# Four seams of a four-layer network: inverse sums by block transpositions, a query bank, queued maxima and reordered pooling products

## Chip, cores and metric

The kernel runs on one core of a Trainium2 chip. The metric is the device time of one execution in microseconds (us); lower is better. The engines are TensorE (PE in the profile; its weight loads are PEld), VectorE (DVE), ScalarE (ACT), GpSimd (POOL) and SyncE (SP), which issues the DMAs. A core has one of each, and they run their own instruction queues in order, held together by semaphores.

## What is computed

The reference sends two images of 512 channels and 64 x 64 pixels, in fp32, through four residual layers. Each adds a function of the group-normalised input (32 groups) to the input:

```python
x = x + _L0_conv_ref(_gn(x), ...)   # local 3x3 attention with pooled keys
x = x + _L1_conv_ref(_gn(x), ...)   # attention on keys sampled at learnt offsets
x = x + _L2_conv_ref(_gn(x), ...)   # mixture of max pools of sizes 1, 3, ... 13
x = x + _L3_conv_ref(_gn(x), ...)   # linear attention with random features
```

The change touches layers 1 and 2. Layer 1, in short, for each of 8 heads of 64 channels:

```python
q   = einsum('oc,bchw->bohw', w_q, x)
off = tanh(w_off2 @ gelu(q[::4, ::4] * w_off1 + b_off1)) * 4
kv  = w_kv @ grid_sample_bilinear(q, grid + off)     # 16 x 16 = 256 keys
out = w_out @ (softmax(q * 64**-0.5 @ k.T) @ v) + b_out
```

The softmax runs over 256 keys; its denominators are sums of exponentials, one for each head and token. Layer 2 takes the mean of each channel, maps the means through two small matrices to one number per channel, and mixes two neighbouring pool sizes by it:

```python
s = relu(w2 @ relu(w1 @ mean(x) + b1) + b2); q_s = clip(floor(s), 0, 5)
out = (s - q_s) * pool[q_s + 1] + (q_s + 1 - s) * pool[q_s] + x
```

A max pool of size 2j+1 is the 3 x 3 maximum applied j times, and the kernel uses that.

## The kernel before

The two images run one after the other, each through the four layers. An image lies in SBUF as `X`, 128 partitions x 4 channel groups (`cc` or `oc`, 0 to 3) x 4096 pixels; a second such tile, `Y`, takes queries, attention results or maxima. A block (`blk`) is 512 pixels, so there are 8 blocks. PSUM has 8 banks of 128 x 512 fp32; most are rented from rotating pools under the name `mm`. An fp32 matmul appears as two MATMUL records (passes).

The order of the instructions on each engine is set by the framework's scheduler: it simulates the program, starts on each engine the instruction that comes earliest in program order among those that are ready, and then adds the semaphores. Where the code says `manual_schedule(engines=...)`, the named engine keeps the program's order. `issue_after(ins)` orders all instructions of its block on the engine of `ins` behind `ins`, without a semaphore.

**Layer 1, start** (`query_and_sample`, from line 1281). Four banks of the pool `pp` (4 in all) hold the first products for the offsets, 256 columns each; Gelu (line 1255) reads them. `acc` is a tile of four banks of its own. Its banks 0 and 1 serve `shift_columns` (lines 992 to 1009), which makes the query bias `bq`, its bank 2 the last moments (`stats_in_steps`, lines 960 to 973). Later all four gather the sampled features (line 1342). The weights are copied to `wq` by GpSimd (line 1317). `query(0)` then makes the first queries: for each channel group 4 matmuls (`project`, line 134) into a bank, and line 1296 adds the bias. Its first bank comes from `pp`.

**Layer 1, attention** (`layer1`, from line 1037). A loop runs over 32 steps (block, channel group), with later stages some steps behind: exponentials (1495 to 1501), products with the values (1510), once per block `inverse_sums` (1514 to 1527), then `divided` (1534 multiplies out the inverses over the channels, 1537 applies them), then the output product of one channel group per step (`add_output`, 1222 to 1232). In `inverse_sums` the sums of the 8 heads lie in one bank `psD`: in each strip of 32 partitions the even rows hold one head's sums, the odd rows the other's, and `divided` uses only the first two rows of each strip.

In the last block each output group is followed by `bn_aggr` (1116), the mean and variance of the group's channels. Between these stand pieces of layer 2's first 3 x 3 maxima (`maxima_across`, `maxima_down`, `across_rows`, lines 1135 to 1164, the last through `spread_max`, line 698), work for VectorE. Then `pool_mixture` (1180 to 1220) makes the mixture's weights from the means: its first matmul is line 1187, its first VectorE instruction 1189.

**Layer 2** (`layer2`, `pool_chunk`, from line 1358). For each channel group, VectorE makes the pools j = 2 to 6 one out of the other, in two steps each: `spread_max` along x into the scratch `h`, then along y into the next pool. Line 698 does the inner columns or rows on VectorE, 699 the two edges on ScalarE. TensorE adds the weighted pools: `product(b, dg, src, j)` (1403) multiplies block b of pool j with a diagonal matrix (1408, ScalarE) into the accumulator bank `accs[b]`.

In the last group (`cc == KC - 1`) VectorE's order is the program's own. There, the group statistics of the first three channel groups, which layer 3 needs, are made alongside, in the accumulator of the last block, `accs[NB - 1]`: `stats_in_steps` is a generator, and its first step (965 to 968) runs after pool 4, its second (970 to 973) after pool 5. Until then the products of the last block are kept in the list `kept`; they are issued at j = 5, after its block 3. GpSimd's power at 973 gives the scale `rstd`, by which line 1433 (ScalarE) scales layer 3's weights.

Of the kernel before, what the change touches and what calls it, by code (L numbers as in the profile page):

```python
# [9 lines left out]
F32 = mybir.dt.float32  # L10
# [923 lines left out]
class Net(General):  # L934
# [22 lines left out]
        for _ in self.stats_in_steps(ks, pp.tile([P, TB], F32, name="mm") if ps is None else ps):  # L957
            pass

    def stats_in_steps(self, ks, ps):  # L960

        nc, mv = self.nc, self.mv
        nmean, rstd, cent, var = (self.stats[:, i, ks] for i in range(4))
        n = ks.stop - ks.start
        nc.tensor.matmul(ps[:, :n], self.grp, mv[:, ks, 0], start=True, stop=True)
        nc.vector.tensor_tensor(cent, mv[:, ks, 0], ps[:, :n], ALU.subtract)
        nc.vector.tensor_tensor(var, cent, cent, ALU.mult)
        nc.vector.tensor_tensor(var, var, mv[:, ks, 1], ALU.add)
        yield
        nc.tensor.matmul(ps[:, KC:KC + n], self.grp, var, start=True, stop=True)  # L970
        nc.scalar.mul(nmean, ps[:, :n], -1.0)
        nc.vector.tensor_scalar(var, ps[:, KC:KC + n], 1e-5, None, ALU.add)  # L972
        nc.gpsimd.tensor_tensor(rstd, var, self.mhalf[:, :n], ALU.pow)  # L973
# [63 lines left out]
    def layer1(self, X, Y, d):  # L1037
# [6 lines left out]
        with tc.tile_pool(name="l1", bufs=1) as sp:  # L1044
# [13 lines left out]
            with tc.tile_pool(name="l1c", bufs=1) as late:  # L1058

                keys = late.tile([P, KC, NK], F32, name="keys")  # L1060
                vals = late.tile([P, 2, C], F32, name="vals")
                with tc.tile_pool(name="l1q", bufs=4, space=PSUM) as pp:
                    for oc in range(KC):
                        ps = pp.tile([P, TB], F32, name="mm")
                        for kc in range(KC):
                            nc.tensor.matmul(ps[:, :NK], wkv[:, kc, oc * P:(oc + 1) * P],
                                             feats[:, kc, :], start=(kc == 0), stop=(kc == KC - 1))
                        nc.scalar.mul(keys[:, oc, :], ps[:, :NK], HD ** -0.5)
                    for t in range(2):
                        ps = pp.tile([P, TB], F32, name="mm")  # L1070
                        for kc in range(KC):
                            nc.tensor.matmul(ps, feats[:, kc, t * P:(t + 1) * P], wkv[:, kc, C:],
                                             start=(kc == 0), stop=(kc == KC - 1))
                        nc.vector.tensor_copy(vals[:, t, :], ps)
                    self.product_bound(top, keys, sp, pp)
                with tc.tile_pool(name="l1b", bufs=2) as wp, \
                        tc.tile_pool(name="l1s", bufs=6, space=PSUM) as pp, \
                        tc.tile_pool(name="l1o", bufs=2, space=PSUM) as ppo:
                    st = wp.tile([P, KC, NB, 6], F32, name="gn_st1", bufs=1)
                    w1 = wp.tile([P, KC, 32], F32, name="w1", bufs=1)  # L1080
                    nc.sync.dma_start(w1, d["w1"].rearrange("(kc p) e -> p kc e", p=P))
                    w2 = wp.tile([32, C], F32, name="w2", bufs=1)
                    nc.sync.dma_start(w2, d["w2"])
                    wo = wp.tile([P, KC, C], F32, name="wo1", bufs=1)
                    nc.sync.dma_start(wo, d["w_out1"].rearrange("(kc p) o -> p kc o", p=P))
                    steps = [(blk, cc) for blk in range(NB) for cc in range(KC)]
                    part = lambda blk, cc=slice(0, KC): Y[:, cc, blk * TB:(blk + 1) * TB]
                    flat = lambda a: a.rearrange("p k o -> p (k o)")
                    probs, totals, later = {}, {}, []
                    rows3 = self.scratch[:, :KC * 10 * W].rearrange("p (k y x) -> p k y x", k=KC, x=W)  # L1090
                    ring = cycle([a[:, n:n + TB] for a, lo, hi in (
                        (flat(wq), 0, KC), (flat(wkv), 5, 8), (flat(feats), 0, 2),
                        (wp.tile([P, 3 * TB], F32, name="totals", bufs=1), 0, 3))
                        for n in range(lo * TB, hi * TB, TB)]).__next__
                    for i in range(len(steps) + 4 + KC):
                        if i < len(steps):
                            blk, cc = steps[i]
                            probs[i], totals[i] = self.exponentials(part(blk, cc), keys[:, cc, :],
                                                                    ring, wp, pp)
                        if 1 <= i <= len(steps):  # L1100
                            blk, cc = steps[i - 1]
                            self.attended(part(blk, cc), probs.pop(i - 1),
                                          vals[:, :, cc * P:(cc + 1) * P], ppo)
                        at = lambda n: i >= n and (i - n) % KC == KC - 1 and (i - n) // KC
                        if (blk := at(1)) is not False and blk < NB:
                            r = self.inverse_sums([totals.pop(KC * blk + n) for n in range(KC)], wp,
                                                  pp)
                        if (blk := at(2)) is not False and blk < NB:
                            self.divided(part(blk), r, pp)
                        if (blk := at(3)) is not False and blk < NB:  # L1110
                            later += [(blk, oc) for oc in range(KC)]
                        if later:
                            blk, oc = later.pop(0)
                            self.add_output(X, wo, part(blk), blk, oc, st, pp)
                            if blk == NB - 1:
                                nc.vector.bn_aggr(self.mv[:, oc, :],
                                                  st[:, oc].rearrange("p b s -> p (b s)"))
                                if oc < 2:
                                    self.maxima_across(X, NB - 2, rows3, slice(oc, oc + 1))
                                    self.maxima_down(Y, NB - 2, rows3, slice(oc, oc + 1))  # L1120
                                for rows in ([(20, 32), (32, 44)], [(10, 20), (44, 55)],
                                             [], [])[oc]:
                                    self.across_rows(Y, slice(*rows))
                            elif oc == KC - 1 and blk < NB - 2:
                                self.maxima_across(X, blk, rows3, slice(0, KC))
                                self.maxima_down(Y, blk, rows3, slice(0, KC))
                    mixture = self.pool_mixture(w1, w2, wp, pp)
                    next(mixture)
                    self.maxima_across(X, NB - 1, rows3, slice(0, 1))
                    self.maxima_down(Y, NB - 1, rows3, slice(0, 1))  # L1130
                    for rows in (0, 10), (55, W):
                        self.across_rows(Y, slice(*rows))
                    next(mixture)

    def maxima_across(self, X, blk, h, ks):
# [145 lines left out]
    def query_and_sample(self, X, Y, wq, bq, grid, feats, top, wp, pp, ppk):  # L1281
# [9 lines left out]

        def query(blk):
            for cc in range(KC):
                ps = pp.tile([P, TB], F32, name="mm")
                self.project(ps, wq[:, :, cc * P:(cc + 1) * P], X, blk)
                nc.scalar.activation(Y[:, cc, blk * TB:(blk + 1) * TB], ps, AF.Identity,
                                     bias=bq[:, cc:cc + 1])
# [88 lines left out]
    def pool_chunk(self, X, Y, cc, c0, d0, wts, sp):  # L1386
# [7 lines left out]
            self.pools.insert(0, Y[:, cc - 1, :])  # L1394
        h = image(self.scratch)
        accs, kept = self.accs, []
        stats = self.stats_in_steps(slice(0, KC - 1), accs[NB - 1])
        if cc == KC - 1:
            self.diags = cycle([next(self.diags), next(self.diags),
                                *[sp.tile([P, P], F32, name=f"diag{i}") for i in range(2, 7)]])  # L1400
# [5 lines left out]
        def add(w, src, j):  # L1406
            dg = next(self.diags)
            nc.scalar.activation(dg, self.ident, AF.Copy, scale=w)  # L1408
            for b in range(NB):
                if b == NB - 1 and cc == KC - 1 and j < 5:  # L1410
                    kept.append((b, dg, src, j))
                else:
                    product(b, dg, src, j)
                while kept and j == 5 and b == 3:
                    product(*kept.pop(0))

        add(c0[:, cc:cc + 1], x2, 0)
        flat = Y[:, cc, :]
        for j in range(1, 7):
            if j > 1:  # L1420
                last, flat = image(flat), self.pools.pop(0)
                self.pools.append(flat)
                if cc or j > 2:
                    self.spread_max(h, last, 2)
                self.spread_max(image(flat), h, 1)
                if cc == KC - 1 and j in (4, 5):
                    next(stats, None)
                if cc == KC - 1 and j == 3:
                    self.moments(sp)
                if cc == KC - 1 and j == 5:  # L1430
# [83 lines left out]
    def inverse_sums(self, totals, wp, pp):  # L1514
# [6 lines left out]
                                 self.cst[:, C_EVEN + h:C_EVEN + h + 32], totals[cc][h],  # L1521
                                 start=(h == 0), stop=(h == 1))
        r = wp.tile([P, TB], F32, name="recip")
        for i in range(2):
            half = slice(i * TB // 2, (i + 1) * TB // 2)
            nc.vector.reciprocal(r[:, half], psD[:, half])
        return r

    def divided(self, att, r, pp):
# [1373 lines left out]
```

## Time and profile before

| what | value |
|---|---|
| median of 3 timed runs | 4915.69 us (4914.85 to 4920.11) |
| profiled execution, its own time | 4912.44 us |
| its span, first to last instruction | 4910.6 us |
| mean granted TensorE clock | 0.989 |
| MATMUL records / VectorE instructions | 16883 / 4044 |
| first image: layer 1, layer 2, layer 3 begin at | 1009, 1482, 1682 us |
| second image: layer 0, 1, 2, 3 begin at | about 2471, 3449, 3917, 4116 us |

The profile's views that are used: the page (busy share of each engine), the list of waits (who waited for whom: total, times, longest), the timeline (start, duration, engine, line, operation, tiles, and in brackets the idle time before it and what ended it), the rows of one line (durations in ns as min/median/max), and tables of stretches (busy time of each engine in a stretch, then the granted clock, the DMA engines' share and GB/s). Times count from the span's start. A wait for several semaphores is put down to the one that came last.

### The profile page before, as it was taken

The page shows a single profiled execution, that of the slowest core. Times are in us where ns is not written, and L with a number is a line of the kernel's source. Part 1 is how long each engine was busy: PE and PEld are TensorE (multiplying, and loading weights), DVE is VectorE, ACT ScalarE, POOL GpSimd, SP SyncE. Part 2 cuts the span into 40 slices and gives each one's busy share as a digit, 9 for nine tenths or more (in the row PEclk, how much of TensorE's full clock was granted, in tenths as well). Part 3 has the DMA queues.
Part 4 walks back from the last instruction along what each step waited for, and adds up shares of the span by engine and source line. Part 5 has one row for each costly group of instructions (what it writes and reads, how often), then busy time and mean ns, then how long its engine had stood idle before and what let it go on. Part 6 is the DMA issues. An engine that isn't in the chain of part 4 may idle for free. (4 is left out here: it accounts for less than half of the span.)

```text
span 4910.6 us, 48474 instructions
## 1 busy us (share of the span) xinstructions
PE 4726.7 (96%) x16883; PEld 1965.5 (40%) x16883; DVE 2983.6 (61%) x4044; ACT 1851.7 (38%) x3555; POOL 1815.6 (37%) x1164
## 2 busy tenths in 40 slices
PE   7999999999999999999999999999999999999999
PEld 3433332555334444433344333325543344444333
DVE  4267777754679633377633677777536795334766
ACT  1256665334323233323212566652443233333222
POOL 0036666501320045545400466665013201454544
PEclk9999999999999999999999999999999999999999
DMA  4035556600000000111120455565000000000111
GB/s 157 1 94 156 154 157 169 178 24 10 1 0 19 1 1 1 56 55 56 65 78 2 108 156 157 156 172 160 20 10 1 2 17 1 1 1 18 44 50 46
DMA packets 129441, 313.30 MB, mean 64 GB/s; under 512 B 23394, under 2 KB 36194, under 8 KB 127652
## 3 DMA queue, kind: packets, MB, share of 16 engines
q1 hardware_dynamic: 129188, 310.12, 21.8%
q8 instruction: 135, 2.21, 0.2%
q14 instruction: 118, 0.97, 0.1%
HBM read 260.73 MB, written 49.31 MB: 63 GB/s over the span
## 5 line engine op out<-in xcount | busy, mean ns | idle before, releaser
L134 PE MATMUL mm<-big,w 128*128 128x512 f32 x2496 | 1157.8, 608 | 19.1 <-DVE big L2485 13.6
L134 PEld LDWEIGHTS mm<-big,w 128*128 128x128 f32 x2496 | 453.1, 191 | 689.7 <-issue 549.0
L2706 POOL TENSOR_TENSOR late<-late,big 128x1024 f32<-128x1024 f32 x194 | 459.2, 2367 | 216.6 <-DVE big L2701 174.4
L1702 POOL TENSOR_TENSOR big<-big 128x512 f32<-128x512 f32 x224 | 277.6, 1271 | 219.3 <-ACT big L1693 219.3
L2526 DVE TENSOR_TENSOR prods<-qs,big 128x2048 f32<-128x2048 f32 (+1 forms) x184 | 330.7, 1819 | 34.3 <-PE tap L2564 23.7
L2701 DVE TENSOR_TENSOR big<-big,mm 128x512 f32<-128x512 f32 x388 | 252.4, 682 | 104.6 <-ACT mm L2693 103.2
L1693 ACT ACTIVATE big<-mm,ed 128x256 f32<-128x256 f32 x512 | 194.1, 490 | 232.7 <-DVE top L1689 200.3
L2693 ACT COPY mm<-big 128x512 f32<-128x512 f32 x432 | 245.4, 597 | 80.3 <-DMA big<-rows 46.1
L2706 POOL TENSOR_TENSOR late<-late,tap 128x1024 f32<-128x1024 f32 x94 | 222.0, 2361 | 97.8 <-DVE tap L2701 83.7
L1501 POOL TENSOR_TENSOR wq<-prob 128x512 f32<-128x512 f32 x48 | 71.9, 1520 | 486.3 <-ACT prob L1498 474.8
L1689 DVE TENSOR_REDUCE top<-mm 128x1 f32<-128x512 f32 x256 | 159.0, 683 | 148.2 <-PE mm L1620 148.2
L2611 POOL TENSOR_TENSOR late<-late 128x512 f32<-128x512 f32 x76 | 95.4, 1275 | 395.7 <-ACT late L2596 379.5
L134 PE MATMUL mm<-big,wq 128*128 128x512 f32 x512 | 235.0, 604 | 2.7 <-ACT off_t L1255 2.7
L1227 PE MATMUL mm<-big,wo 128*128 128x512 f32 x512 | 237.6, 610 | 0.0
L1667 PE MATMUL mm<-w,big 128*128 128x512 f32 x512 | 234.5, 601 | 0.0
L1403 PE MATMUL acc<-big,diag 128*128 128x512 f32 x512 | 227.7, 602 | 5.2 <-ACT diag L1408 4.6
L1961 PE MATMUL mm<-k,w 128*128 128x512 f32 x512 | 232.0, 600 | 0.7 <-DVE big L1964 0.7
L973 POOL TENSOR_TENSOR group_stats<-group_stats,cst 128x1 f32<-128x1 f32 (+1 forms) x20 | 20.2, 1024 | 543.0 <-DVE group_stats L972 489.7
L134 PE MATMUL mm<-big,big 128*128 128x512 f32 x464 | 201.7, 594 | 0.5 <-DVE b_sr L1011 0.5
L1926 POOL TENSOR_SCALAR qf_sum<-qf,ksum_ratio 128x512 f32<-128x512 f32 x64 | 100.4, 1570 | 264.2 <-PE psD L1944 212.4
L1498 ACT ACTIVATE prob<-mm 128x512 f32<-128x512 f32 x256 | 133.3, 602 | 171.3 <-PE mm L1495 171.1
L2564 PE MATMUL tap<-prods,cst 128*32 128x512 f32 x1152 | 183.2, 604 | 11.5 <-DVE prods L2526 7.4
(432 smaller groups left out, 8118.7 us busy)
## 6 DMA issues: line engine op xcount, KB each, us to landing
big<-rows SPq DMA_DIRECT2D x432, 256.0 KB
tap<-rows SPq DMA_DIRECT2D x208, 256.0 KB
yd<-late SPq DMA_DIRECT2D x32, 512.0 KB
lost_all<-lost SPq DMA_DIRECT2D x128, 128.0 KB
out<-big SPq DMA_DIRECT2D x64, 256.0 KB
big<-in_W_kv SPq DMA_DIRECT2D x8, 1024.0 KB
rows<-late SPq DMA_DIRECT2D x64, 128.0 KB
big<-in_x SPq DMA_DIRECT2D x32, 256.0 KB
```

What stands on the lines that cost most here:

```text
L134: self.nc.tensor.matmul(ps, w[:, kc, :], X[:, kc, blk * TB:(blk + 1) * TB], start=(kc == 0), stop=(kc == KC - 1))
L1227: nc.tensor.matmul(ps, w[:, kc, oc * P:(oc + 1) * P], att[:, kc, :], start=(kc == 0), stop=(kc == KC - 1))
L1403: nc.tensor.matmul(accs[b], dg, src[:, b * TB:(b + 1) * TB], start=(j == 0), stop=(j == 6))
L1667: nc.tensor.matmul(ps, X[:, kc, lo:lo + P], wv[:, kc, :], start=(kc == 0), stop=(kc == KC - 1))
L1693: nc.scalar.activation(f[:, t, :], pS[h][i][:, t % 2, :], AF.Exp, bias=ed[:, t, 2 * cc + h:2 * cc + h + 1])
L1702: nc.gpsimd.tensor_tensor(a, a, part, ALU.add)
L1961: nc.tensor.matmul(ps, self.wo[:, kc, oc * P:(oc + 1) * P], qs[:, kc, :], start=(kc == 0), stop=(kc == KC - 1))
L2526: self.nc.vector.tensor_tensor(self.pair(u, k)[:, :n].rearrange("p k (y x) -> p k y x", x=W), bcast(qs.rearrange("p (y x) -> p y x", x=W), ...
L2564: nc.tensor.matmul(ps[32 * q:32 * q + 32, :], self.cst[:, C_TAPW + 16 - 2 * k:][:, :32], self.pair(u, k)[:, 0, j * TB:(j + 1) * TB], start ...
L2693: nc.scalar.copy(ps, part)
L2701: nc.vector.tensor_tensor(part.rearrange("p (y x) -> p y x", x=W), self.vx[:, y:y + self.UY // 2, dx:dx + W], ps.rearrange("p (y x) -> p y ...
L2706: nc.gpsimd.tensor_tensor(out, out, t, ALU.add)
```

## The change

Five edits in four places.

1. `inverse_sums`: the two reciprocals of 256 columns each are replaced by a transposition of `psD` in blocks of 32 x 32, in place; a reciprocal of two columns of each block (16 x 2 = 32 columns); and a transposition back into `r` that reads these two columns 16 times over.
2. `query(0)`: its first product goes into bank 3 of `acc` instead of a bank of `pp`.
3. The two last pieces of `across_rows`, rows 0 to 10 and 55 to 64, are queued on VectorE behind the last `bn_aggr`.
4. `stats_in_steps` has a further stop after its second matmul (line 970), if asked. In the last pooling chunk, both of its matmul steps now stand after pool 4 and ahead of its products; the rest (971 to 973) stands at j = 5 between the two halves of pool 5.
5. The kept products are issued at j = 5 ahead of that pool's own products.

```diff
-    def stats_in_steps(self, ks, ps):
+    def stats_in_steps(self, ks, ps, split=False):
...
         nc.tensor.matmul(ps[:, KC:KC + n], self.grp, var, start=True, stop=True)
+        if split:
+            yield
         nc.scalar.mul(nmean, ps[:, :n], -1.0)
...
-                                nc.vector.bn_aggr(self.mv[:, oc, :],
-                                                  st[:, oc].rearrange("p b s -> p (b s)"))
+                                mean = nc.vector.bn_aggr(
+                                    self.mv[:, oc, :], st[:, oc].rearrange("p b s -> p (b s)"))
...
-                    for rows in (0, 10), (55, W):
-                        self.across_rows(Y, slice(*rows))
+                    with tc.issue_after(mean.ins):
+                        for rows in (0, 10), (55, W):
+                            self.across_rows(Y, slice(*rows))
...
-                ps = pp.tile([P, TB], F32, name="mm")
+                ps = acc[:, KC - 1] if not blk + cc else pp.tile([P, TB], F32, name="mm")
...
-        stats = self.stats_in_steps(slice(0, KC - 1), accs[NB - 1])
+        stats = self.stats_in_steps(slice(0, KC - 1), accs[NB - 1], True)
...
             nc.scalar.activation(dg, self.ident, AF.Copy, scale=w)
+            while kept and j == 5:
+                product(*kept.pop(0))
             for b in range(NB):
                 if b == NB - 1 and cc == KC - 1 and j < 5:
                     kept.append((b, dg, src, j))
                 else:
                     product(b, dg, src, j)
-                while kept and j == 5 and b == 3:
-                    product(*kept.pop(0))
...
+                if cc == KC - 1 and j == 5:
+                    next(stats, None)
                 self.spread_max(image(flat), h, 1)
-                if cc == KC - 1 and j in (4, 5):
-                    next(stats, None)
+                if cc == KC - 1 and j == 4:
+                    next(stats)
+                    next(stats)
...
         r = wp.tile([P, TB], F32, name="recip")
-        for i in range(2):
-            half = slice(i * TB // 2, (i + 1) * TB // 2)
-            nc.vector.reciprocal(r[:, half], psD[:, half])
+        nc.vector.transpose(psD, psD)
+        two = psD.rearrange("p (b n r) -> p b n r", n=16, r=2)[:, :, 0]
+        nc.vector.reciprocal(two, two)
+        nc.vector.transpose(r.rearrange("p (b n r) -> p b n r", n=16, r=2), bcast(two, 2, 16))
         return r
```

## The prediction

> **What bounds the kernel.** I read the page first: the share of each engine, then the clock row. TensorE is busy for nearly the whole span and nothing else comes near, so time is won where TensorE stands still or runs slowly.
>
> ```profile
> PE 4726.7 (96%) x16883; PEld 1965.5 (40%) x16883; DVE 2983.6 (61%) x4044; ACT 1851.7 (38%) x3555; POOL 1815.6 (37%) x1164
> ```
>
> Next the list of who waited for whom, TensorE alone (total us, times, longest). Four of its lines are the places of this change, each met twice, once per image:
>
> ```profile
> PE mm L1187 <- DVE channels_mv L1116: 5.7, 2, 2.8
> PE acc L1403 <- DVE group_stats L972: 5.4, 2, 2.7
> PE mm L1534 <- DVE recip L1526: 4.2, 2, 2.1
> PE mm L134 <- ACT off_t L1255: 2.7, 2, 1.3
> ```
>
> Together 18.0 us, 0.37% of the span. But a stall also costs afterwards. Stretches after the inverse sums of image 0's last block (busy per engine; the number after POOL's is the granted clock):
>
> ```profile
> 1448.00:1449.00 1.00, 0.00 (x0) 0.00 (x0) 1.00 (x1) 0.00 (x0) 0.00 (x0) 1.00 0.00 0
> 1449.00:1450.00 1.00, 0.84 (x8) 0.31 (x8) 0.97 (x3) 0.00 (x0) 0.00 (x0) 0.86 0.00 0
> 1450.00:1451.00 1.00, 1.00 (x5) 0.32 (x2) 0.65 (x2) 0.00 (x0) 0.00 (x0) 0.50 0.00 0
> ...
> 1456.00:1457.00 1.00, 1.00 (x3) 0.50 (x2) 0.00 (x0) 0.00 (x0) 0.00 (x0) 0.73 0.00 0
> ```
>
> After 2.13 us of stall the clock is halved for 0.28 + 6 + 0.54 = 6.8 us. Image 1 has the same stall (2.11) and keeps its clock: from L1534 to the last L1227 it takes 18.50 us, image 0 21.85. So this dip costs 3.35 us. After the L134 stall the first query product likewise takes 5.37 us in image 0 and 3.67 in image 1: 1.70.
>
> **Rule against row.** The Trainium skill, "TensorE: Matmul & The Clock Gate", section "Why this matters for your kernels", asks only that idle gaps stay below about 3 us; by it these gaps of 1.3 and 2.1 us are harmless and parts 1 and 2 lose 5.05 us of worth. The rows show dips, so I count them. The page's Part 1 says that the window (3.4 us) runs freely; that fits one image dipping and the other not, and makes this gain a matter of phase.
>
> **1. Inverse sums.** Two reciprocals at L1526 (1.72 us each, 3.36 for both at 1445.75) become transposition, reciprocal of 32 columns, transposition. The same three stand at L2646 to L2649:
>
> ```profile
> L2646 DVE STREAM_TRANSPOSE mm<-mm x32: 731/731/732, 288.2 to 3371.7; 128x512 f32<-128x512 f32 x32
> ...
> L2648 DVE RECIPROCAL mm<-mm x32: 351/366/367, 289.0 to 3372.9; 128x32 f32<-128x32 f32 x32
> ...
> L2649 DVE STREAM_TRANSPOSE late<-mm x32: 716/717/719, 289.4 to 3373.3; 128x512 f32<-128x512 f32 x32
> ```
>
> 0.731 + 0.366 + 0.717 and two gaps of 0.034 give 1.88: 1.48 less. In 14 of 16 blocks VectorE has slack (psD is ready at 1412.8, L1534 runs at 1420.08), so nothing is won there. In the last block of each image the stall falls from 2.1 to about 0.6: 2 x 1.48 = 2.96, and image 0's dip goes: 3.35. Bound: the two gaps of the chain can take in another instruction, as L1952 enters the chain at L1948 (2.34 us). Only L1230 (0.65) is near ready here; then it is 0.8 per image. I take 1.48, as L1230 comes later in program order.
>
> **2. First query product in a bank of `acc`.** It no longer waits for Gelu (table load 1.28, then 0.56) to free a bank: 1.34 per image, 2.68; its other inputs are ready (last copy of wq ends at 1013.2). It can also fill the 0.75 that TensorE waits for L994 before L1006; between 0 and 0.75 I take 0.5, a bit over one pass of 0.43: 1.0. L1006, bq and Gelu are then up to 0.4 late, covered by the rest of the product (3.4 us). Dip of image 0: 1.70. Sum 5.4. Bank 3 is next written at L1342, well after L1296 has read it.
>
> **3. Maxima's pieces behind the last mean.** At image 0's end of layer 1:
>
> ```profile
> 1470.68 0.80 DVE L698 TENSOR_TENSOR wkv<-big 128x620 f32<-128x620 f32 x1
> ...
> 1471.40 0.74 DVE L1230 SCALAR_TENSOR_TENSOR big<-mm,vec,big 128x512 f32<-128x512 f32 x1
> 1472.06 0.73 DVE L698 TENSOR_TENSOR wkv<-big 128x558 f32<-128x558 f32 x1
> 1472.71 0.69 DVE L1232 BATCH_NORM_STATS2 gn_st<-big 128x6 f32<-128x512 f32 x1
> ```
>
> The last matmul ends at 1471.01. With both pieces gone, L1230, L1232 and L1116 run 1471.08 to 1472.96 (0.75 + 0.69 + 0.37 and gaps) in place of 1473.80: 0.84. The pieces (0.80 + 0.73) now follow the mean. L1189 can start 0.68 to 0.88 after it, so one piece fits (it ends 0.72 after the mean); if both go first, L1189 is 0.5 to 0.7 late. Value between 0.1 and 0.84: 0.4, 0.8 for two. The clock is halved here anyway (the pause is over 8 us).
>
> **4. Last pooling chunk.** TensorE waits from 1660.17 to 1662.86. The named L972 is not the only holder: the product of j = 5 also needs the fifth pool, an L698 that ends at 1662.71.
>
> ```profile
> 1662.86 3.67 PE L1403 MATMUL acc<-pool,diag 128*128 128x512 f32 x8 [2.69 <-DVE group_stats L972]
> 1662.86 4.89 POOL L973 TENSOR_TENSOR group_stats<-group_stats,cst 128x3 f32<-128x3 f32 x1 [185.68 <-DVE group_stats L972]
> ...
> 1667.14 4.29 DVE L698 TENSOR_TENSOR big<-wkv 128x3968 f32<-128x3968 f32 x1
> 1667.78 3.79 ACT L1433 ACTIVATE w<-w,group_stats 128x512 f32<-128x512 f32 x6 [4.56 <-POOL group_stats L973]
> ```
>
> The five kept products (10 passes of 0.429 = 4.3 us) need only L971 and L972. L970 now comes before j = 4's products, so L972 can run at 1658.4, ahead of the fifth pool. Kept products then fill 1660.1 to 1664.4, j = 5 takes 16 passes to 1671.3. Late next is the sixth pool, ready at 1671.43, with j = 6 at about 1671.6 where it is 1674.09: 2.5. One thing takes part of it back: L973 now starts near 1658.7, beside an L698 (4.89 us as today, where the one-column form takes 0.56), so L1433 runs 1663.6 to 1667.4 on ScalarE ahead of the edges of the sixth pool's first half (L699, today 1662.80). Those end at 1667.75, the last L698 starts 0.6 late: 1.9 to 2.0. If L970 stayed behind j = 4's products (1659.89), VectorE would wait 1.9 for L972: 0.6. I take 2.0: 4.0 for two. In layer 2 VectorE runs without a pause of note from 1536 to 1671, so the earlier savings pass through it only because its start (1482) moves with them.
>
> **Sum.** Parts 1 to 4: 6.3 + 5.4 + 0.8 + 4.0 = 16.5. The profiled execution took 4912.44 (span 4910.6 and 1.8 around it) and would take 4895.9. The timed runs' median is 3.25 above it, a difference of the size of one clock dip; I carry it along: 4899.2. Later layers follow TensorE, and no DMA limits a seam (DMA share 0.01 or less in these stretches), so the gains stay.
>
> **Rivals.**
> - Stalls shrink, but the clock takes its share: other seams (1.5 to 1.8 us at 956, 968, 2117, undipped today) meet the windows differently. Without the 5.05: 11.4, 4904.3. For it: one image dips, one doesn't. Against: as many dips can vanish as come.
> - Part 4 turns against itself: POOL's L973 gets through only when VectorE pauses after the next L698 (1667.1); L1433 holds ScalarE to 1671.0, the edges come at 1671.4, the last L698 ends at 1675.8, j = 6 starts 1.8 late. 16.5 - 2 x 3.8 = 8.9: 4906.8. For it: L1433 before the edges in program order; against: L973 needed only one L698 to pass today.
> - Slower: the new chain lets large maxima in. L1143 to L1157 (2.2 to 3.2 us each) enter before it and in both gaps, in the 12 blocks that have them: up to 1.88 + 3 x 3.24 = 11.6 us, against 7.2 from psD to L1534. From 7.2 on TensorE stalls; halfway, 2.7 us in 12 blocks, costs 33: 16 slower, 4932. Against: these maxima end at 1404.7, 8 us before the next psD.
> - That the change does nothing is excluded for part 2: the bank's wait is gone by construction.
>
> **Numbers.** As forecast 0.60 (own range 4895 to 4904), clock rival 0.22, part 4's rival 0.14, slower 0.04. A measurement tells 0.2%, 9.8 us, from no change: the bound is 4905.9. Nearly all of the first case, three quarters of the second and four tenths of the third lie below: faster 0.80, same 0.16, slower 0.04. Low end: fill 1.5, pieces 1.7, part 4 at 5.0 make 18.9, 4896.8, and two dips fewer elsewhere (about 3 each) 4891. High end: third case and a little clock, 4908.
>
> **What would show it.** L134 following L1006 or L994 with no wait on Gelu; L1534's wait near 0.6 and clock 1.00 behind it; L1187's wait near 2.0 to 2.4; kept products at 1660 without a wait, and j = 6 waiting under 1 us on the last L698. L1433 ahead of L699 with VectorE idle, or L1230 within the transpositions, would prove those steps wrong; dips at other seams would make the sum wrong.

## The result, and the profile after

The changed kernel takes 4899.26 us (median of 18 runs, 4895.99 to 4903.53); the kernel before, beside it on the same chip, 4912.43 us (18 runs, 4902.65 to 4920.11). The ratio is 0.9975, 95% interval 0.9969 to 0.9981. By the means of these runs the change is worth 12.6 +- 1.2 us. The profiled execution fell from 4912.44 to 4899.03 us: 13.4.

The page's first line, and then the list of waits of TensorE (total us, times, longest), of the changed kernel:

```profile
PE 4718.9 (96%) x16883; PEld 1963.8 (40%) x16883; DVE 2958.2 (60%) x4060; ACT 1849.4 (38%) x3555; POOL 1815.3 (37%) x1164
```

```profile
PE mm L1190 <- DVE channels_mv L1118: 4.0, 2, 2.0
...
PE mm L2302 <- DMA prods<-yd: 2.9, 4, 1.1
...
PE mm L1197 <- DVE pool_var L1194: 2.8, 2, 1.4
...
PE mm L1541 <- DVE recip L1533: 1.3, 2, 0.6
...
PE acc L1406 <- DVE big L698: 1.0, 2, 0.5
```

TensorE does the same 16883 passes in 7.8 us less busy time: that is half clock that has gone, since a pass at half clock counts double. All lines but L2302's are what the four seams still cost. Two of the old waits are smaller, L1190's (it was L1187's 5.7) and L1541's (it was L1534's 4.2); the 5.4 for the kept products is off the list; three are larger or new: L1197's (L1194's 1.7 before), L1406's on line 698, and L2302's at the output of layer 0, which the change doesn't touch.

To account for all of it I used two sums from the trace: the time between its first and its last matmul in which TensorE runs none, and the time that half clock costs (half of the busy time under a clock record of one half). The span less these two is 4717.7 us before and 4718.4 after, so they explain all but 0.7 of the difference:

| TensorE, both images, us | forecast | before | after | gained |
|---|---|---|---|---|
| 1. inverse sums, idle | 2.96 | 4.23 | 1.25 | 2.98 |
| 2. query bank, idle | 3.7 | 2.67 | 0.83 | 1.84 |
| 3. pieces, idle at two matmuls | 0.8 | 5.68 + 1.70 | 3.96 + 2.75 | 0.67 |
| 4. kept products, idle ahead of j = 5 and of j = 6 | 4.0 | 5.38 + 0 | 0 + 1.01 | 4.37 |
| half clock behind parts 1 and 2 | 5.05 | 3.41 + 1.71 | 0 | 5.12 |
| idle elsewhere | 0 | | | -4.1 |
| half clock elsewhere | 0 | | | 3.2 |
| sum | 16.5 | | | 14.1 |

Most of the idle time elsewhere is at the output of layer 0, where TensorE waits for DMAs after the change (line 2302: its idle time rose by 1.31 in image 0 and by 1.62 in image 1). In image 0 the wait stands where half clock stood before (at 900 us, cost 2.93): TensorE came there sooner and had to wait. In all fourteen profiles of this document no image with that dip has such a wait, and seven of the nine images without the dip have it. The half clock elsewhere is a balance of many dips: those at 900, 3409 and 4877 us went (7.6), new ones came at 1690, 3616, 4124 and 4541 (6.6), and others changed in length.

Part 1. VectorE's timeline (start, duration, engine, line, tiles) of the changed kernel in the last block of image 0:

```profile
1440.13 0.69 DVE L1148 TENSOR_TENSOR wkv<-wkv,big 128x512 f32<-128x512 f32 x1
1440.74 0.72 DVE L1530 STREAM_TRANSPOSE mm<-mm 128x512 f32<-128x512 f32 x1
1441.50 0.37 DVE L1532 RECIPROCAL mm<-mm 128x32 f32<-128x32 f32 x1
1441.90 0.72 DVE L1533 STREAM_TRANSPOSE recip<-mm 128x512 f32<-128x512 f32 x1
1442.54 0.71 DVE L1233 SCALAR_TENSOR_TENSOR big<-mm,vec,big 128x512 f32<-128x512 f32 x1
```

The chain ends at 1442.62, 1.88 us after its start, with nothing in its two gaps. The stretches behind it (busy per engine; the number after POOL's is the granted clock) show no dip:

```profile
1442.00:1443.00 1.00, 0.38 (x5) 0.31 (x8) 1.00 (x2) 0.00 (x0) 0.00 (x0) 1.00 0.00 0
1443.00:1444.00 1.00, 1.00 (x9) 0.26 (x2) 0.97 (x3) 0.00 (x0) 0.00 (x0) 1.00 0.00 0
1444.00:1445.00 1.00, 1.00 (x3) 0.42 (x3) 1.00 (x2) 0.00 (x0) 0.00 (x0) 1.00 0.00 0
1445.00:1450.00 5.00, 5.00 (x13) 2.24 (x12) 4.96 (x9) 0.43 (x2) 0.00 (x0) 1.00 0.00 0
```

Part 2. TensorE's timeline at the start of layer 1; in brackets the idle time and what ended it:

```profile
1012.25 1.06 PE L994 MATMUL acc<-big,group_stats 128*32 128x512 f32 x8
1014.07 1.05 PE L1008 MATMUL acc<-cst,hatx 128*128 128x1 f32 x8 [0.75 <-ACT hatx L996]
1015.53 3.67 PE L134 MATMUL acc<-big,wq 128*128 128x512 f32 x8 [0.41 <-DVE bq L1011]
```

L134 still comes after L1008, so the 0.75 stays open. And it waits for L1011 on VectorE, the copy that reads `bq` out of another bank of the same tile `acc`.

Part 3. VectorE at the end of layer 1:

```profile
1462.73 0.37 DVE L1118 BATCH_NORM_AGGREGATE channels_mv<-gn_st 128x2 f32<-128x48 f32 x1
1463.02 0.74 DVE L698 TENSOR_TENSOR wkv<-big 128x620 f32<-128x620 f32 x1
1463.78 0.16 DVE L1192 TENSOR_TENSOR pool_cent<-channels_mv,mm 128x4 f32<-128x4 f32 x1
1463.86 0.73 DVE L698 TENSOR_TENSOR wkv<-big 128x558 f32<-128x558 f32 x1
1464.51 0.16 DVE L1193 TENSOR_TENSOR pool_var<-pool_cent 128x4 f32<-128x4 f32 x1
```

The first piece fits behind the mean. The second slipped in behind L1192 and holds L1193 back. TensorE's second matmul of the seam, before and then after, waits 1.38 where it waited 0.85:

```profile
1475.29 0.59 PE L1194 MATMUL mm<-pool_var,cst 128*128 128x4 f32 x2 [0.85 <-DVE pool_var L1191]
...
1464.91 0.39 PE L1197 MATMUL mm<-pool_var,cst 128*128 128x4 f32 x2 [1.38 <-DVE pool_var L1194]
```

Part 4. ScalarE, and then TensorE, in the last pooling chunk:

```profile
1652.21 3.79 ACT L1439 ACTIVATE w<-w,group_stats 128x512 f32<-128x512 f32 x6 [4.69 <-POOL group_stats L975]
1655.90 0.39 ACT L699 COPY wkv<-pool 128x128 f32<-128x128 f32 x1
```

```profile
1653.23 7.03 PE L1406 MATMUL acc<-pool,diag 128*128 128x512 f32 x16
1660.77 3.67 PE L1406 MATMUL acc<-big,diag 128*128 128x512 f32 x8 [0.51 <-DVE big L698]
```

The weights' scaling stands ahead of the edge copy, as the forecast had it; VectorE loses 0.46 to it, and j = 6 waits 0.51. The 2.69 ahead of j = 5 is gone.

### The profile page after: what moved, and what is told of

Its sections match the earlier page's. It is cut to its first block, busy times and chain, and to the rows that moved or that the text cites. A ratio compares the mean times of both kernels' runs of the same rounds, so it can differ in the third digit from the quotient of the medians.

```text
span 4897.2 us, 48490 instructions
## 1 busy us (share of the span) xinstructions
PE 4718.9 (96%) x16883; PEld 1963.8 (40%) x16883; DVE 2958.2 (60%) x4060; ACT 1849.4 (38%) x3555; POOL 1815.3 (37%) x1164
## 5 line engine op out<-in xcount | busy, mean ns | idle before, releaser
L134 PE MATMUL mm<-big,w 128*128 128x512 f32 x2496 | 1157.7, 608 | 19.1 <-DVE big L2492 13.6
L134 PEld LDWEIGHTS mm<-big,w 128*128 128x128 f32 x2496 | 452.9, 191 | 689.7 <-issue 549.0
L1406 PE MATMUL acc<-big,diag 128*128 128x512 f32 x512 | 227.7, 602 | 6.2 <-ACT diag L1411 4.6
L134 PE MATMUL mm<-big,wq 128*128 128x512 f32 x496 | 226.0, 600 | 0.0
L134 PE MATMUL mm<-big,big 128*128 128x512 f32 x464 | 201.7, 594 | 0.5 <-DVE b_sr L1013 0.5
```

Of the source, the lines that this page charges most:

```text
L134: self.nc.tensor.matmul(ps, w[:, kc, :], X[:, kc, blk * TB:(blk + 1) * TB], start=(kc == 0), stop=(kc == KC - 1))
L1406: nc.tensor.matmul(accs[b], dg, src[:, b * TB:(b + 1) * TB], start=(j == 0), stop=(j == 6))
```

## Experiments

Two questions were open: are the parts worth in time what the trace shows of their stalls, and when does a stall cost half clock as well? "Stalls" below means idle time alone, "phase" that the clock adds to it or not, by where the stall lies against the windows of the clock (they are worked out below). Means of runs are given with one standard error.

**Part 1 alone.** The kernel before with only this:

```diff
-        for i in range(2):
-            half = slice(i * TB // 2, (i + 1) * TB // 2)
-            nc.vector.reciprocal(r[:, half], psD[:, half])
+        nc.vector.transpose(psD, psD)
+        ...
```

> The kernel before with the inverse sums by block transpositions and nothing else. Theory 'stalls and phase': the wait on the inverse sums falls from 2.1 to about 0.6 us in each image (3.0 us together), and the clock dips that followed it in about half of the executions (3.35 us each, two images) go as well, on average another 3.4: about 6.4 us faster than before, with less spread between executions than before. Theory 'stalls only' (dips go and come elsewhere): 3.0 us faster and the same spread.

4910.03 us median (mean 4909.3 +- 1.2) beside 4911.86 (mean 4911.9 +- 0.8); ratio 0.9996, 0.9988 to 1.0005. The idle time of this seam fell by 2.99 (2.98 in the full change). The time fell by 2.6 +- 1.4: that agrees with the stall; 6.4 lies 2.7 standard errors away, and the runs scatter as before's do (standard deviation 4.3 and 4.5). The dip of this seam went, but the profile has others at 1657 and 1698 that before's lacks. The 3.35 was not a steady worth.

**Part 2 alone.**

```diff
-                ps = pp.tile([P, TB], F32, name="mm")
+                ps = acc[:, KC - 1] if not blk + cc else pp.tile([P, TB], F32, name="mm")
```

> The kernel before with the first query product in bank 3 of acc and nothing else. In the changed kernel this product waits 0.41 us, for the copy of the query bias on VectorE, and follows L1006 instead of filling the pause before it. So the stall falls by 0.93 us per image, 1.9 together. Theory 'stalls and phase': with dips of 1.7 us in about half the cases, 3.5 us faster. Theory 'stalls only': 1.9.

4905.82 us (mean 4905.7 +- 0.8) beside 4911.86: 6.2 +- 1.1 less; ratio 0.9989, 0.9980 to 0.9997. The stall gave 1.84 of it. Of the clock: in the five profiles that have the old query stall (before, part 1 alone, part 3 alone, part 4 alone twice) a dip of 1.71 follows in 9 of 10 images; in the nine with the new bank, in none of 18. That makes 2 x 0.9 x 1.71 = 3.1, and 4.9 together, within the error. So here the clock's part is real, and larger than the one dip of the forecast.

**Part 3 alone.** One run.

```diff
+                    with tc.issue_after(mean.ins):
+                        for rows in (0, 10), (55, W):
+                            self.across_rows(Y, slice(*rows))
```

> The kernel before with the maxima's last pieces queued behind the last mean and nothing else. Both theories: the wait before pool_mixture's first matmul falls from 2.84 to about 2.0 us, the one before its second rises from 0.85 to about 1.4 because the second piece stands between its VectorE instructions; 0.3 us per image in all. A theory that the pieces are free behind the mean expects 0.84 and no rise.

4917.67 us, one run, which tells nothing of 0.6 us. Its seam: 5.68 to 3.95 and 1.70 to 2.75, as in the full change: 0.3 per image.

**Part 4 alone**, that is the changed kernel with the other three places as before.

> The changed kernel with parts 1 to 3 undone: only the kept products ahead of the sixth pool's own ones, and the statistics a half pool earlier. Both theories: the 2.69 us wait goes, about 0.5 comes back before the last pool's products, 2.2 us per image, 4.4 together and no clock dip involved: 4.4 us faster, the spread of before unchanged.

4910.95 us (mean 4912.0 +- 1.1) beside 4911.86 (mean 4911.9 +- 0.8): nothing, though its trace has the stalls 4.39 lower. This was a miss, and it was taken up again below.

**How long a stall halves the clock?** The changed kernel, with up to 11 more transpositions in place ahead of the reciprocal (an even number, or an even number and a product by 1.0), another number in each block, so that one run has stalls of many lengths:

```diff
+        more = [9, 10, 10, 11, 9, 10, 10, 0, 10, 9, 11, 10, 10, 9, 11, 0][self.calls % 16]
+        for _ in range(more // 2 * 2):
+            nc.vector.transpose(psD, psD)
+        if more % 2:
+            nc.vector.tensor_scalar(psD, psD, 1.0, None, ALU.mult)
```

> The changed kernel with 9, 10 or 11 further in-place transpositions (the odd one a multiplication by 1) in the inverse sums of 14 blocks, which make TensorE wait some 1.5 to 3 us before the inverse's products in each of them; the result is unchanged. Theory 'phase': whether a dip follows depends on where the 3.41 us windows fall; a stall of about 2.2 us is followed by a dip in about half the blocks, one of 3 us in most, one of 1.5 us in few or none, and the dips start on one fixed grid. Theory of the rule (gaps under about 3 us are harmless): no dip after any stall under 3 us.

> The same with another order of lengths, for 14 more stalls. Expectations as for the first: by 'phase' a stall's dip follows from how much of one window it empties, with one threshold of idle time for both kernels; by the rule none under 3 us.

Spans 4934.7 and 4939.3. Two stalls of the same 2.28 us in the first of the two, both read from the stretches; the first pair of numbers is the stretch:

```profile
3743.00:3744.00 1.00, 0.08 (x2) 0.00 (x0) 0.96 (x2) 0.59 (x1) 0.00 (x0) 1.00 0.00 0
3744.00:3745.00 1.00, 0.00 (x0) 0.00 (x0) 0.93 (x3) 0.00 (x0) 0.00 (x0) 1.00 0.00 0
3745.00:3746.00 1.00, 0.64 (x4) 0.52 (x8) 0.31 (x1) 0.00 (x0) 0.00 (x0) 0.71 0.00 0
3746.00:3747.00 1.00, 1.00 (x8) 0.00 (x0) 0.00 (x0) 0.00 (x0) 0.00 (x0) 0.50 0.00 0
```

```profile
1328.00:1329.00 1.00, 0.00 (x0) 0.00 (x0) 0.93 (x3) 0.03 (x1) 0.00 (x0) 1.00 0.00 0
1329.00:1330.00 1.00, 0.35 (x4) 0.31 (x8) 0.60 (x1) 0.00 (x0) 0.00 (x0) 1.00 0.00 0
1330.00:1331.00 1.00, 1.00 (x9) 0.28 (x2) 0.19 (x1) 0.00 (x0) 0.00 (x0) 1.00 0.00 0
```

After the first the clock is halved, after the second it stays at 1.00. The difference is the grid. In each profile all dips of the clock record begin on one grid of 3.413 us, to 0.002 us over the whole span; a window is the time between two lines of it. The first stall lies whole within one window of it; of the second, at most 1.40 us lies in one. Of all stalls over 0.6 us before the inverses' product, in all fourteen profiles of this document (56), none of the 43 that have 1.95 us or less in a single window halved the clock, and all 13 with 2.11 or more did. In each of the 13 the half clock begins at the end of that window. So a stall of 2.12 us, the one that part 1 shortens, dips only if it lies almost whole in one window: it did in 7 of 10 cases.

**Part 4 on top of the others, and three ways to shift layer 3.** In the profiles up to here, the start of layer 3 (pauses of 0.68, 0.67 and 1.03 us at L987, L1008 and L1020, with passes of one column between) had a dip in 7 of 8 images of the kernels with part 4 and 1 of 8 of the others. Four kernels on one chip; the edits to the changed kernel are: part 4 undone; the scaling put behind the edge copies (`scale_ahead` holds the loop of L1439); two more matmuls ahead of layer 3's first products; none.

```diff
+                if cc == KC - 1 and j == 6:
+                    with self.tc.issue_after(edge[1].ins):
+                        self.scale_ahead()
```

```diff
+        for ps in first[:2]:
+            nc.tensor.matmul(ps, wk[:, 0, :P], X[:, 0, :TB], start=True, stop=True)
         self.first_products(first, wk, X[:, :, :TB], slice(0, KC - 1))
```

> The changed kernel with part 4 alone undone (parts 1 to 3 stay). Stalls alone: TensorE's idle time at that seam comes back, 5.4 us, and the wait for the sixth pool's product falls by 1.0; the time is 4.4 us above the changed kernel's (about 4904). Phase theory (the clock is judged in windows of 3.413 us on a fixed grid, and the profiles so far show the small pauses at layer 3's start dipping when the one before L1018/L1020 begins 2.95 to 3.41 or 0 to 0.81 us after a grid line, not at 1.31 to 2.63): part 4 moves that seam 2.2 us earlier and so into the dip, 1.7 us per image; without part 4 the seam begins near 1.8 to 2.4, no dip at 1690 and 4124, and the time is only about 1.0 us above the changed kernel's (about 4900.5).

> The changed kernel with the scaling of layer 3's weights (L1439) ordered behind the edge copies of the sixth pool's first half. Both theories: VectorE's 0.46 before the last L698 and TensorE's 0.51 before the product of j = 6 go, in each image. Stalls alone: 0.9 faster than the changed kernel, the dips at layer 3's start stay. Phase theory: layer 3's start moves 0.46 earlier, from 2.99 to about 2.53 after a grid line in image 1, where there is no dip (1.7 more won), and from 0.16 to about 3.1 in image 0, where the dip stays: 2.6 faster.

> The changed kernel with two more fp32 matmuls of 128x512 ahead of layer 3's first products in each image, whose result is written over: 1.76 us more work per image, the output is the same. Stalls alone (or dips by chance): 3.5 us slower. Phase theory: they move the seam at layer 3's start from 2.99 and 0.16 to about 1.35 and 1.9 after a grid line, where no dip has been seen; the 1.7 us of dip per image go, and the time is within 0.5 us of the changed kernel's.

> The changed kernel itself, beside the other three on one chip. Both theories: 4899 to 4900. Phase theory: dips at layer 3's start near 1690 and 4124 in this profile too (the grid's phase at the kernel's start differs, but from 250 us on it is the same to 0.2 us in all eight profiles so far); by chance: 1 in 4 to 1 in 2 per image.

| kernel | median | mean | L1020 (L1018 without part 4) starts, us after a grid line (image 0, 1) | dip |
|---|---|---|---|---|
| part 4 undone | 4902.68 | 4903.3 +- 0.8 | 1.04, 1.76 | none |
| scaling behind the edges | 4898.76 | 4899.1 +- 1.1 | 2.37, 1.98 | none |
| two more matmuls | 4907.89 | 4907.3 +- 0.8 | 0.70, 0.69 | both |
| the change again | 4899.96 | 4899.6 +- 1.3 | 2.42, 2.37 | none |

(The expectations give the same instant, though they speak of the pause's beginning.) The rule of phase held in all eight new cases: 0.70 and 0.69 dipped, 1.04 to 2.42 didn't. But what was built on it fell. The change again met the seam at 2.4, not at 0.16 and 2.99, so its phase there is no property of the kernel. Part 4 on top of parts 1 to 3 is worth 3.7 +- 1.5 by the means and 2.7 by the medians, nearer to its stalls (4.4) than to 1.0. Two matmuls of 3.5 us in all cost 7.7 +- 1.5. Their profile has the seam at 0.7 and a dip of two windows there:

```profile
1695.00:1700.00 5.00, 5.00 (x6) 2.04 (x7) 0.69 (x1) 0.97 (x2) 2.95 (x3) 0.50 0.00 0
1700.00:1701.00 1.00, 1.00 (x3) 0.34 (x2) 0.00 (x0) 0.00 (x0) 0.00 (x0) 0.51 0.00 0
```

With 1694 to 1695 and 1700 to 1701 this dip costs 3.06, and one in image 1 as much. These two and the matmuls make 9.6; other seams gave some of it back, and in the whole profile half clock costs only 1.4 more than in that of the change again. The scaling behind the edges gained only 0.5 +- 1.7: it now stands ahead of the second edge copy, and VectorE's last L698 waits 0.45 for that instead; TensorE's wait fell from 1.0 to 0.7 for both images together, not to 0.

**Part 4 alone once more, and the three refinements.** The latter is the changed kernel with the edit above and two more: the accumulator as four tiles, and the two pieces behind L1212, in the pause ahead of `pool_s`.

```diff
-        acc = ppk.tile([P, KC, TB], F32, name="acc")
+        acc = [ppk.tile([P, TB], F32, name=f"acc{i}") for i in range(KC)]
...
-                    with tc.issue_after(mean.ins):
+                    next(mixture)
+                    with tc.issue_after(self.weighed.ins):
                         for rows in (0, 10), (55, W):
-                            self.across_rows(Y, slice(*rows))
-                    next(mixture)
+                            piece = self.across_rows(Y, slice(*rows))
+                    with tc.issue_after(piece.ins):
+                        next(mixture)
```

> Part 4 alone once more, since it brought nothing alone (4912.0 mean beside 4911.9) and 3.7 on top of parts 1 to 3. If nothing is what part 4 alone brings, because it carries layer 3's seam into a dip from the phase that the kernel before has: the same mean as before within 1.5 us, and dips at layer 3's start again in both images. If the first was a poor draw of phases: 2 to 5 us below before; the profile's layer 3 seam dips only where it begins 2.95 to 3.41 or 0 to 0.81 us after a grid line.

> The changed kernel with three refinements: the banks of the key stage's accumulator are four tiles instead of one (so the first query product waits for no reader of another bank), maxima's two pieces stand in the 2.8 us pause after L1212 instead of around L1191, and L1439 stands behind the edge copies of the sixth pool's first half. Stalls by the trace of the changed kernel: 0.41 + 0.75, about 0.5 (1.38 before L1193 back to 0.85) and 0.51 per image, in all 2 x 2.2 = 4.3 us: 4895 to 4896. If dips decide (layer 3's seam at 0 to 0.81 or 2.95 to 3.41 after a grid line dips, at 1.0 to 2.65 it doesn't): between 4892 and 4900, with the seams' idle time gone all the same.

Part 4 alone: 4914.61 us (mean 4913.4 +- 0.8) beside 4915.45 (mean 4913.9 +- 1.0). Nothing again: 0.2 +- 0.9 less over both sets of runs. Its idle time is 4.0 lower than before's, and the dip at layer 3's start is there in both images, with the seam at 2.98 and 2.98 (2.97 and 3.00 the first time). The stretches of this kernel:

```profile
1699.00:1700.00 1.00, 0.12 (x1) 0.13 (x2) 0.00 (x0) 1.00 (x3) 1.00 (x2) 1.00 0.00 0
1700.00:1701.00 1.00, 1.00 (x2) 0.51 (x3) 0.00 (x0) 0.99 (x2) 1.00 (x2) 0.65 0.00 0
1701.00:1702.00 1.00, 1.00 (x2) 0.34 (x1) 0.41 (x1) 0.00 (x0) 1.00 (x2) 0.50 0.00 0
1702.00:1703.00 1.00, 1.00 (x2) 0.34 (x1) 0.28 (x1) 0.00 (x0) 0.93 (x1) 0.50 0.00 0
1703.00:1704.00 1.00, 1.00 (x3) 0.51 (x2) 0.00 (x0) 0.00 (x0) 0.00 (x0) 0.64 0.00 0
```

and the same place in the second profile of the full change:

```profile
1692.00:1693.00 1.00, 0.15 (x1) 0.15 (x2) 0.00 (x0) 1.00 (x3) 1.00 (x2) 1.00 0.00 0
1693.00:1694.00 1.00, 1.00 (x3) 0.52 (x4) 0.00 (x0) 0.96 (x2) 1.00 (x2) 1.00 0.00 0
1694.00:1695.00 1.00, 1.00 (x3) 0.38 (x3) 0.69 (x1) 0.00 (x0) 1.00 (x2) 1.00 0.00 0
```

The instructions are the same; above, two of TensorE's passes per microsecond, here three. This dip takes back 2 x 1.71 = 3.4 of the 4.4. All 28 cases of this seam in the fourteen profiles obey one rule: no dip where L1020 starts 1.04 to 2.79 us after a grid line (16), a dip where it starts later than 2.94 or before 0.82 (12). That part 4 alone brings nothing because of this dip is thus supported by two sets of runs, but not shown: in the two profiles half clock costs 8.6 and 9.0 us more than in before's, of which this dip is 3.4, and the rest lies at other seams. Nor are the four images four separate draws, since from 870 to 2077 us the two profiles meet the windows alike to 0.02 us.

The three refinements: 4896.37 us (mean 4895.0 +- 1.4, 5 runs) beside 4915.45; ratio 0.9959, 0.9945 to 0.9973. Against the change's 0.9975 that is some 4.6 us more by the means over all runs (4899.6 to 4895.0, on different chips), where 4.3 were expected, with an error of about 1.5. TensorE's timeline at the query seam and at the end of layer 1:

```profile
1016.95 1.13 PE L134 MATMUL acc<-big,wq 128*128 128x512 f32 x2
1017.91 0.95 PE L1008 MATMUL acc<-cst,hatx 128*128 128x1 f32 x8
1018.72 2.82 PE L134 MATMUL acc<-big,wq 128*128 128x512 f32 x6
...
1465.08 0.39 PE L1192 MATMUL mm<-channels_mv,cst 128*128 128x4 f32 x2 [1.98 <-DVE channels_mv L1118]
1466.32 0.39 PE L1199 MATMUL mm<-pool_var,cst 128*128 128x4 f32 x2 [0.85 <-DVE pool_var L1196]
```

With four tiles the first product does fill the pause ahead of L1008, and both waits there are gone; the second matmul at layer 1's end is back at 0.85.

## Why the prediction was right, and where its terms were not

The end value fits: 4899.2 forecast, 4899.26 measured, and the direction too. That the four seams cost TensorE what their rows show, and give it back, was right. That the value fits so closely is luck, since two errors cancel: the sum was 16.5 and the profiles' difference 13.4; and the 3.25 that I carried along, because the three runs shown lay above the profiled execution, was not there: the median of 18 runs of before is 4912.43, the profiled execution's own 4912.44.

- **Step 1**: 2.96 forecast, 2.98 measured, chain 1.88 as worked out from the three rows; nothing came in between. The dip in image 0 went. But its 3.35 is a share of phases, not a fixed worth: alone, part 1 gave 2.6.
- **Step 2**: the 0.5 for the fill was 0, and of the 1.34 the step gave 0.92. Both have one cause: the new bank is part of the same tile, so L134 has to wait for L1011, the copy of `bq` out of a neighbouring bank. That copy comes behind L1008, so L134 can't go ahead of L1008, and it waits 0.41 behind it. I had thought of bank 3's later writer and not of its neighbours' reader; with four tiles both losses went. That makes 1.84 for 3.7. The 1.70 for its dip was too small on the mean: 3.1 by the ten images above.
- **Step 3**: 0.4 per image, 0.3 measured. The first wait fell by 0.86, the most that was forecast. "If both go first" was not what happened: the second piece went behind L1192 (L1189 before) and cost 0.53 at the next matmul.
- **Step 4**: the best of them: 2.69 gone, L1439 ahead of the edge copies, the last L698 late by 0.46 (0.6 forecast), 2.2 per image for 2.0. What the step lacked is layer 3, 30 us on, where the same passes can run at half clock; I counted that among other seams and gave it 0.
- **Sum**: stalls 9.9 for 11.45, clock behind the parts 5.12 for 5.05, elsewhere -0.9 for 0. "DMA share 0.01 or less in these stretches" is not so at the query seam, where before has a share of 1.00 from 1012 to 1014 us; no wait of that seam names a DMA, but the output of layer 0 waited for one after the change. The clock rival's mechanism (other seams meet the windows differently) fits part 4 alone, which gained nothing. In the full change one profile has the dips at layer 3's start (1.62 and 1.71), the other has none, and the runs give part 4 there 3.7 +- 1.5.
- **Rule against row**: the Trainium skill ("TensorE: Matmul & The Clock Gate", "Why this matters for your kernels") asks only that idle gaps stay below about 3 us. Here 13 stalls with 2.11 us or more in one window all halved the clock, nine of them shorter than 3 us, and seven of only 2.11 to 2.13. The row was the better guide, and counting a dip of one profile at full price, as I did, was too bold.
- The other two rivals: no large maximum came into the transpositions' chain, and POOL's power took 4.89 us from 1647.29, as before: it ended 0.71 us after the first L698 that it met, and had no need of a second.

## What to carry to other kernels

A stall of TensorE has two prices: its length, which a trace gives to 0.1 us, and the half clock behind it, which depends on where it lies against a free-running grid; take the first from the row, the second as a price times a chance from several profiles (which can repeat one another), and look at the next short pauses downstream before you count a gain in full. When a result goes into another bank of a tile that is already in use, ask who reads and writes the other banks of that tile; separate tiles took that wait away here. A piece of work queued "behind X" can still land between X's two next followers: place it in a pause that is longer than the piece.

## What the runs showed of the hardware

- **The clock's windows lie on a fixed grid** of 3.413 us in all fourteen profiles; where it starts against the kernel differs from run to run (the first instruction lies 0.10 to 2.94 us after a grid line).
- **What halves the clock**: of the stalls ahead of the inverses' product, all 13 with 2.11 us or more within one window did, and none of the 43 with 1.95 or less; nothing between was met.
- **The kernel falls into step with this grid.** The start of five passes of TensorE, in us after a grid line, over the fourteen profiles (the arc is the shortest stretch of the window that holds them all):

| pass number | at about | arc of the 14 starts |
|---|---|---|
| 1 | 25 us | 2.76 |
| 201 | 99 us | 1.58 |
| 401 | 176 us | 0.63 |
| 601 | 250 us | 0.21 |
| 2401 | 757 us | 0.22 |

  The spread shrinks where passes run at half clock: over the first long passes, up to 37 us, from 2.76 to 1.58 (they take up to 1.06 us each, then 0.59; the clock record begins there); behind the dip at 166 us to 0.63; behind that at 193 us to 0.21. The dip at 250 us leaves it, and so do the stretches at full clock. A likely reason, not tested: work that restarts early runs at half clock until the same grid line as work that restarts late, so a lead is partly lost. In image 1 it is the same: the arc is 1.5 at 2604 us and 0.2 at 2678. So some dips, as those at 166, 193 and 250 us, are in every profile here; that a gain ahead of such a place is partly taken back would follow, but was not tried.
- **It can fall out of step again.** The two profiles of the changed kernel meet the windows alike to 0.02 us from 214 to 783 us. Behind 900 us, where one has a dip and the other waits for DMAs, they are 0.81 apart, and at layer 3's start they differ as told above.
- **Short pauses add up within a window.** Layer 3's start has no pause over 1.03 us and dips all the same. Idle time alone does not sort the 28 cases: a window with 1.03 us of it had a dip behind it in some and none in others. Idle time and passes of one column taken together do: none of the 16 whose fullest window has 1.72 us or less of them dipped, and all 12 with 1.88 or more did, at the end of that window. So these passes seem to count little or nothing as work; no run tried them by themselves.
- **GpSimd's power on 128 x 3** took 4.89 us beside one of VectorE's long L698, where the one-column form takes 0.56 elsewhere. In all 28 cases it began 0.12 us after an L698 of 4.29 and ended 0.71 after that one's end, so these runs can't tell whether it was slow or waited for VectorE.
